# Graph attention layers: turn the state first, multiply by weights that carry two score columns, then attend; slope of the scores on ScalarE

## The chip, the cores and the metric

The kernel runs on one core of one Trainium2 chip, in one launch. The metric is the device time of the whole program in microseconds (us). The engines are named as in the profile: PE (TensorE, matrix products), PEld (its weight loads), DVE (VectorE), ACT (ScalarE), POOL (GpSimd) and SP (SyncE, which issues all DMAs here). Everything is computed in f32.

## What is computed

128 independent graphs have 128 nodes with 256 features each. Three attention layers follow one another, each with its own weights `W` and score vector `a`, and then a gated graph network with three steps:

```python
h = jnp.maximum(_layernorm(x, axis=-1), 0.0)
x = x + _L0_gnn_ref(h, adj, L0_gnn_W, L0_gnn_a)      # layers 1 and 2 alike

# _L0_gnn_ref(x, adj, W, a)
Wh = jnp.einsum('bnf,fo->bno', x, W)
a1, a2 = (a[:F_out, 0], a[F_out:, 0])
e = (Wh @ a1)[:, :, None] + (Wh @ a2)[:, None, :]
e = jnp.where(e > 0, e, ALPHA * e)                   # ALPHA = 0.2
attention = jnp.where(adj > 0, e, NEG_BIG)
attention = jax.nn.softmax(attention, axis=-1)
h_prime = jnp.einsum('bij,bjo->bio', attention, Wh)
return jax.nn.elu(h_prime)

# layer 3, three times: m = h @ weight[i]; aggr = A^T m; h = GRU(aggr, h)
```

## The kernel before

**Tiles and groups.** The graphs are taken in 33 groups: two graphs in the first and the last, four in the others (`SIZES`, L217). A tile has the nodes or the features on its 128 partitions. `gat(g)` (L670) loads a group's `x` and `adj`, makes the mask `cap` (a very large number where there is an edge, minus it elsewhere) and runs `attention(g, l, ...)` (L491) three times; it then normalises once more and turns the state so that the features are on the partitions (`h`). `gru(g, ...)` (L736) runs three steps with 24 products of 512 columns each (L790, names `nn`, `r`, `z`, `ni`) and the aggregation (`agp`, L813), writes the result and the output. A turned copy of the state for the next step (`hn`) goes out to DRAM and back through `turned_state` (L469).

**One attention layer** (group of n graphs). `stats` (L414) gives mean and 1/deviation on DVE and POOL. ACT makes `xn = relu((x - mean) * rs)` (L507). The scores are made from `xn` without the product `Wh`: at the start `attention_weights` (L286) computes `va = W a` for both halves of `a` on DVE (L304), spreads it over the partitions with PE transposes (`vp`, L309) and an ACT copy (L316), and each graph then costs two DVE instructions that multiply `xn` by `va` and sum along the row into `e` (L515). One of the two score columns must lie along the row: `de` takes it to DRAM (L537) and `er` brings it back to all partitions (L539). DVE adds both scores and takes the minimum with `cap` (L557), applies the slope with a second instruction (L569, maximum of em and 0.2 em) and takes the negative row maximum (L571); ACT computes the exponential with its row sum (L575); DVE divides (L582, L586). The attention matrix is turned through DRAM by `exchanged` (L438: DVE transposes 32 x 32 blocks, one DMA writes, four DMAs read back, `at`). PE multiplies `xn` by the attention matrix (`ahp`, L627: 8 products of 128 columns for four graphs), ACT copies the sum to SBUF (`ah`, L634), and PE multiplies it by `W` (`hp`, L646: two k halves of 256 columns per graph). The elu and the sum with x are L660, L662 and L664.

**Near and far.** Groups 0 and 1 are "near" (`FAR = 2`, L216): there, turning is done by PE transposes into PSUM (`e`, `atp`) in place of trips through DRAM, and `rs` is multiplied in later (L515, L606). All other groups are "far".

**The order of the work** is made once, when the program is built. `Plan` (L40) collects every instruction with its engine, an assumed duration and a rank; `issue` (L108) walks through time, gives each engine the lowest rank among what is ready within 0.1 us, holds back whatever is more than 6.0 ranks ahead, and lets an instruction start only when the ring of its buffers (mostly 2) has a free slot. Group g has the ranks 3g to 3g + 3 for its gates, and its attention starts `lead(g)`, 6.5 to 9.5, before that (L926), 2 ranks to a layer. DMAs are planned at 250 KB/us, one behind another, and 1.9 us (L162). The chip then runs each engine's list strictly in that order, each instruction waiting for its semaphores; SP's list of DMAs as well.

**PSUM.** Eight banks: two for everything of the attention (`gat`), five for the gates, one for turning (L235).

Of the kernel before, what the change touches and what calls it, by code (L numbers as in the profile page):

```python
# [8 lines left out]
FT = mybir.dt.float32  # L9
# [176 lines left out]
def kernel(  # L186
# [97 lines left out]
    W, VA = [], []  # L284

    def attention_weights(l, w, a):  # L286
        rank = 1.5 * l - 8.0
        wt, va = const_val(f"w_{l}", [KD, D]), const_val(f"va_{l}", [2, D])
        first = l - 11.2
        load(256, first, lambda: nc.sync.dma_start(  # L290
            wt.t, w.rearrange("(k p) o -> p k o", p=P)), writes=[wt])
        ar = val(su, "ar", [2 * D], f"ar_{l}")
        load(2, first - 0.1, lambda: nc.sync.dma_start(
            ar.t[:1, :], a.rearrange("n o -> o n")), writes=[ar])

        ab = bank("gat", f"ab_{l}")
        add("PE", pe(T), rank, lambda: nc.tensor.matmul(
            ab.t, ones[:1, :], ar.t[:1, :], start=True, stop=True), reads=[ar], writes=[ab])
        wa = val(su, "wa", [2, KD], f"wa_{l}")
        vp = bank("gat", f"vp_{l}")  # L300

        def one(s, k):
            scr = val(su, "scr", [D], f"scr_{l}_{k}_{s}")
            add("DVE", dve(D) + 0.08, rank, lambda: nc.vector.scalar_tensor_tensor(  # L304
                scr.t, wt.t[:, k, :], 1.0, ab.t[:, s * D : (s + 1) * D], op0=OP.mult, op1=OP.mult,
                accum_out=wa.t[:, s, k : k + 1],
            ), reads=[wt, ab], writes=[scr, (wa, (s, k))])
            c = s * KD + k
            add("PE", 0.11, rank, lambda: nc.tensor.transpose(  # L309
                vp.t[:, c * P : (c + 1) * P], wa.t[:, s, k : k + 1].to_broadcast([P, P]), ident  # L310
            ), reads=[(wa, (s, k))], writes=[(vp, c)])

        for s in range(2):
            for k in range(KD):
                one(s, k)
        add("ACT", act(T), rank, lambda: nc.scalar.copy(  # L316
            va.t.rearrange("p s d -> p (s d)"), vp.t), reads=[vp], writes=[va])
        W.append(wt)
        VA.append(va)
# [118 lines left out]
    def exchanged(srcs, cut, dst, name, n, rank):  # L438
# [7 lines left out]
            dram, f"d{kd}_{n}", 2,  # L446
            lambda: dram.tile([Q, 32, Q, f], FT, tag=f"d{kd}_{n}", name=f"d_{name}"),
# [21 lines left out]
    def turned_state(src, dst, name, n, rank):  # L469


        tr = val(gw, "trs", [G, P], f"tr_{name}", cut=n)
        d = plan.val(
            dram, f"ds_{n}", 2, lambda: dram.tile([n, P, P], FT, tag=f"ds_{n}", name=f"d_{name}")
        )
        add("DVE", dve(n * P), rank, lambda: nc.vector.transpose(
            tr.t.rearrange("p b j -> p (b j)"), src.t[:, : n * P]
        ), reads=[src], writes=[tr], takes=[d, dst])
        load(64 * n, rank, lambda: nc.sync.dma_start(d.t.rearrange("b p f -> p b f"), tr.t),
            reads=[tr], writes=[d])  # L480

        def back(j):
            load(16 * n, rank, lambda: nc.sync.dma_start(
                dst.t[j * 32 : (j + 1) * 32, : n * P].rearrange("c (m r) -> c m r", r=32),
                d.t[:, :, j * 32 : (j + 1) * 32].rearrange("b (q c) r -> c (b q) r", q=Q),
            ), reads=[d], writes=[(dst, j)])

        for j in range(Q):
            back(j)

    def attention(g, l, xt, cap, xo):  # L491

        name, n = f"{g}_{l}", SIZES[g]
        rank = 3.0 * g - lead(g) + 2.0 * l
        xn = val(gw, "xn", [G, D], f"xn_{name}", cut=n)
        e = val(gw, "e", [2, G], f"e_{name}")
        far = g >= FAR
        nm, rs = stats(xt, n, name, rank, [xn, e, xo, cap])


# [5 lines left out]
        def centred(b):  # L506
            add("ACT", 0.45, rank, lambda: nc.scalar.activation(  # L507
                xn.t[:, b, :], xt.t[:, b, :], AF.Relu, bias=nm.t[:, b : b + 1],
                scale=rs.t[:, b : b + 1] if far else 1.0,
            ), reads=[(xt, b), nm, *([rs] if far else [])], writes=[(xn, b)])  # L510


        def score(b, s):
            scr = val(gw, "scr", [D], f"scr_{name}_{b}_{s}")
            add("DVE", dve(D), rank, lambda: nc.vector.scalar_tensor_tensor(  # L515
                scr.t, xn.t[:, b, :], 1.0 if far else rs.t[:, b : b + 1], VA[l].t[:, s, :],
                op0=OP.mult, op1=OP.mult, accum_out=e.t[:, s, b : b + 1],
            ), reads=[(xn, b), rs, VA[l]], writes=[scr, (e, (s, b))])

        for b in range(n):  # L520
            centred(b)
        for b in range(n):
            score(b, 1)
            score(b, 0)
# [3 lines left out]

        em = val(gw, "em", [G, N], f"em_{name}", cut=n)
        if far:
            de = plan.val(
                dram, f"de{n}", 2, lambda: dram.tile([P, n], FT, tag=f"de{n}", name=f"de_{name}")
            )
            er = val(gw, "er", [N * G], f"er_{name}")
            load(2, rank, lambda: nc.sync.dma_start(de.t, e.t[:, 1, :n]),  # L537
                reads=[(e, (1, b)) for b in range(n)], writes=[de], takes=[er, em])
            load(64 * n, rank, lambda: nc.sync.dma_start(  # L539
                er.t[:, : N * n], de.t.rearrange("p n -> (p n)").partition_broadcast(P)  # L540
# [4 lines left out]
        def row(b):  # L545
            add("PE", 0.11, rank, lambda: nc.tensor.transpose(
                e2.t[:, b * P : (b + 1) * P], e.t[:, 1, b : b + 1].to_broadcast([P, P]), ident
            ), reads=[(e, (1, b))], writes=[(e2, b)], takes=[em])

        def e2_row(b):  # L550
            if far:
                return er.t[:, : N * n].rearrange("p (i b) -> p b i", b=n)[:, b, :]
            return e2.t[:, b * P : (b + 1) * P]


        def masked(b):
            add("DVE", dve(P) + (0.15 if far else 0.05), rank, lambda: nc.vector.scalar_tensor_tensor(  # L557
                em.t[:, b, :], e2_row(b), e.t[:, 0, b : b + 1],
                cap.t[:, b, :], op0=OP.add, op1=OP.min,
            ), reads=[er if far else (e2, b), (e, (0, b)), cap], writes=[(em, b)])  # L560
# [3 lines left out]
        for b in range(n):  # L564
            masked(b)
# [3 lines left out]
        add("DVE", dve(n * P), rank, lambda: nc.vector.scalar_tensor_tensor(  # L569
            em.t, em.t, ALPHA, em.t, op0=OP.mult, op1=OP.max), reads=[em], writes=[em])  # L570
# [18 lines left out]

        if far:  # L590

            at = val(gw, "at", [Q, G * 32], f"at_{name}")
            exchanged([em], lambda k: em.t, at, f"at_{name}", n, rank)
        else:
            atp = bank("gat", f"atp_{name}")
            at = val(gw, "at", [G, N], f"at_{name}", cut=n)
# [6 lines left out]
        if not far:  # L603
            for b in range(n):
                turn(b)
            add("DVE", dve(n * P), rank, lambda: nc.vector.tensor_tensor(  # L606
                at.t, atp.t[:, : n * P].rearrange("p (g i) -> p g i", g=n),
                rs.t.rearrange("p (g o) -> p g o", o=1).to_broadcast([P, n, N]), op=OP.mult,
            ), reads=[atp, rs], writes=[at])

        def turned_weights(b):
            if far:
                return at.t[:, :, : n * 32].rearrange("p q (b c) -> p b q c", b=n)[:, b]
            return at.t[:, b, :]

        def summed(ps, b):
            o = ps.t[:, b * P : (b + 1) * P]
            return o.rearrange("p (q c) -> p q c", q=Q) if far else o


        ah = val(gw, "ah", [KD, T], f"ah_{name}")

        def gathered(k):
            ps = bank("gat", f"ahp_{name}_{k}")

            def product(b):
                add("PE", pe(P), rank, lambda: nc.tensor.matmul(  # L627
                    summed(ps, b), xn.t[:, b, k * P : (k + 1) * P], turned_weights(b),
                    start=True, stop=True,
                ), reads=[(xn, b), at], writes=[(ps, b)], takes=[ah])  # L630

            for b in range(n):
                product(b)
            add("ACT", act(n * P), rank, lambda: nc.scalar.copy(  # L634
                ah.t[:, k, : n * P], ps.t[:, : n * P]), reads=[ps], writes=[(ah, k)])

        for k in range(KD):
            gathered(k)

        def pair(j):  # L640
# [3 lines left out]
            def product(b, k):  # L644
                c = 2 * j + b
                add("PE", pe(D), rank, lambda: nc.tensor.matmul(  # L646
                    hp.t[:, b * D : (b + 1) * D], ah.t[:, k, c * P : (c + 1) * P],
                    W[l].t[:, k, :], start=(k == 0), stop=(k == KD - 1),
                ), reads=[(ah, k), W[l]], writes=[hp], takes=[t])

            for b in range(2):
                for k in range(KD):
                    product(b, k)
# [16 lines left out]
    def gat(g):  # L670
# [54 lines left out]
        if g == 0:  # L725
# [5 lines left out]
            [hn] * KD, lambda k: hn.t[:, :, k * P : (k + 1) * P], hT, f"h_{g}", n, rank  # L731
# [4 lines left out]
    def gru(g, xt, am, hn0, h0):  # L736
# [36 lines left out]
        def step(i):  # L773
# [50 lines left out]
            def half(c):  # L824
# [58 lines left out]
                if i < STEPS - 1 and FAR <= g < NG - FAR:  # L883
                    ahead.append(state(f"hn{c}", f"hn_{g}_{i + 1}_{c}"))
                    turned_state(hc, ahead[c], f"hn_{g}_{i + 1}_{c}", n_g, quick)
# [11 lines left out]
        if far:  # L897
            exchanged(
                h, lambda k: h[k].t[:, :TG].rearrange("p (b j) -> p b j", b=n_g),
                o, f"o_{g}", n_g, rank,  # L900
# [68 lines left out]
```

## Time and profile before

| | |
|---|---|
| runs of the kernel, median (lowest to highest) | 2757.47 us (2755.29 to 2758.84), 3 runs |
| profiled execution, first to last instruction | 2756.0 us; 1.5 us below the runs' median, no other time is recorded for it |
| busy: PE, PEld | 2712.8 us (98%), 1569.7 us (57%) |
| busy: DVE, ACT, POOL | 2082.3 us (76%), 1280.4 us (46%), 293.7 us (11%) |
| granted PE clock, mean | 0.996 |
| DMA | 503,094 packets, 245.30 MB, 33.5% of 16 engines on the one queue of SP |
| chain of work that ended last | PE 88%, DVE 8%, ACT 2%, DMA 1% |

A line of the groups gives source line, engine, operation, what is written and read, the shapes, the count, then busy us, the mean ns of one, and the idle time of the engine just before them with what ended it. An f32 product stands as two instructions on PE. Matmuls overlap in the pipeline, so the mean of one is longer than the distance between two starts.

### The profile page before, as it was taken

How to read it: one execution, taken by the hardware profiler on the slowest of the kernel's cores; microseconds unless marked ns; L12 is line 12 of the kernel's file. 1: busy time of each engine (PE TensorE's matmuls, PEld its weight loads, DVE VectorE, ACT ScalarE, POOL GpSimd, SP SyncE). 2: the span in 40 equal slices, each digit the busy share in tenths (PEclk: the TensorE clock that was granted, in tenths of full speed). 3: DMA queues.
4: the chain of work that ended last, by engine and by line, in shares of the span. 5: the costliest groups of instructions: out<-in, count | busy, mean ns of one | idle time of the engine just before them, and what ended most of it. 6: DMA issues, size and time to landing. Idle time of an engine off the chain costs nothing.

```text
span 2756.0 us, 32248 instructions
## 1 busy us (share of the span) xinstructions
PE 2712.8 (98%) x9563; PEld 1569.7 (57%) x9563; DVE 2082.3 (76%) x5541; ACT 1280.4 (46%) x2709; POOL 293.7 (11%) x369
## 2 busy tenths in 40 slices
PE   7899999999999999999999999999999999999998
PEld 4755555555555555555555555555555555555546
DVE  7778888778768887877788687778768886876643
ACT  4545444444444454444454445444444444444433
POOL 1111110101101101110111111111101010100000
PEclk9999999999999999999999999999999999999999
DMA  3113334433324433333333344323334333333310
GB/s 91 51 58 100 88 95 101 111 94 86 97 80 108 108 99 78 101 91 96 105 97 83 87 105 104 109 75 91 97 88 110 103 93 86 94 74 93 79 44 12
DMA packets 503094, 245.30 MB, mean 89 GB/s; under 512 B 280580, under 2 KB 472068, under 8 KB 502919
## 3 DMA queue, kind: packets, MB, share of 16 engines
q1 hardware_dynamic: 502918, 243.25, 33.5%
q8 instruction: 76, 1.25, 0.2%
q14 instruction: 100, 0.81, 0.1%
HBM read 139.28 MB, written 103.87 MB: 88 GB/s over the span
## 4 chain that ended last, share of the span: by engine, by line
PE 88%; DVE 8%; ACT 2%; DMA 1%; issue 1%; POOL 0%; SPq 0%; DVEq 0%; ACTq 0%; POOLq 0%
PE z L790 21%; PE r L790 21%; PE hp L646 11%; PE ni L790 11%; PE nn L790 10%; PE ahp L627 6%; PE agp L813 5%; DVE em L557 1%; DVE scr L515 1%; DVE xo L662 1%; DVE xo L664 1%; DVE d L877 1%; ACT em L575 1%; DVE h L880 1%; DVE n L856 0%
## 5 line engine op out<-in xcount | busy, mean ns | idle before, releaser
L790 PE MATMUL nn<-h,whh 128*128 128x512 f32 (+1 forms) x792 | 395.6, 581 | 1.9 <-DVE h L880 1.9
L790 PE MATMUL r<-ag,wc 128*128 128x512 f32 (+1 forms) x792 | 395.2, 581 | 1.3 <-ACT ag L821 1.3
L790 PE MATMUL ni<-ag,wc 128*128 128x512 f32 (+1 forms) x792 | 394.4, 579 | 1.4 <-ACT ag L821 1.4
L790 PE MATMUL z<-ag,wc 128*128 128x512 f32 (+1 forms) x792 | 394.2, 579 | 0.0
L790 PE MATMUL z<-h,whh 128*128 128x512 f32 (+1 forms) x792 | 394.2, 579 | 0.0
L790 PE MATMUL r<-h,whh 128*128 128x512 f32 (+1 forms) x792 | 394.2, 579 | 0.0
L851 DVE SCALAR_TENSOR_TENSOR n<-r,wn 128x512 f32<-128x512 f32 (+1 forms) x198 | 132.6, 670 | 336.5 <-ACT r L848 336.0
L646 PE MATMUL hp<-w,ah 128*128 128x256 f32 x1536 | 373.2, 381 | 0.5 <-ACT ah L634 0.2
L646 PEld LDWEIGHTS hp<-w,ah 128*128 128x128 f32 x1536 | 290.1, 190 | 131.4 <-issue 95.7
L515 DVE SCALAR_TENSOR_TENSOR scr<-xn,va 128x256 f32<-128x256 f32 x732 | 266.4, 423 | 33.9 <-ACT xn L507 33.6
L848 ACT ACTIVATE r<-r,brz 128x512 f32<-128x512 f32 (+1 forms) x198 | 133.2, 673 | 284.3 <-PE r L790 282.0
L813 PEld LDWEIGHTS agp<-am,hn 128*128 128x128 f32 x1536 | 202.3, 191 | 85.7 <-issue 73.5
L790 PEld LDWEIGHTS ni<-ag,wc 128*128 128x128 f32 x792 | 149.8, 190 | 177.9 <-issue 171.0
L790 PEld LDWEIGHTS r<-h,whh 128*128 128x128 f32 x792 | 149.3, 190 | 169.4 <-issue 162.8
L790 PEld LDWEIGHTS z<-h,whh 128*128 128x128 f32 x792 | 148.7, 190 | 168.3 <-issue 158.3
L821 ACT COPY ag<-agp 128x512 f32<-128x512 f32 (+1 forms) x198 | 113.0, 571 | 263.2 <-PE agp L813 262.8
L790 PEld LDWEIGHTS z<-ag,wc 128*128 128x128 f32 x792 | 148.4, 190 | 142.4 <-issue 138.2
L575 ACT ACTIVATE em<-em,nmx 128x128 f32<-128x128 f32 x384 | 149.4, 391 | 168.2 <-DVE nmx L571 166.4
L790 PEld LDWEIGHTS r<-ag,wc 128*128 128x128 f32 x792 | 146.1, 190 | 135.4 <-issue 120.5
L627 PEld LDWEIGHTS ahp<-at,xn 128*128 128x128 f32 x1536 | 191.3, 195 | 49.4 <-issue 37.6
L813 PE MATMUL agp<-am,hn 128*128 128x128 f32 x1536 | 205.3, 275 | 6.4 <-ACT hn L802 3.9
L526 POOL TENSOR_SCALAR xo<-xo 128x1024 f32<-128x1024 f32 (+1 forms) x66 | 73.2, 1110 | 1215.6 <-DVE xo L664 989.8
(94 smaller groups left out, 3474.1 us busy)
## 6 DMA issues: line engine op xcount, KB each, us to landing
d_hn<-tr_hn SPq DMA_DIRECT2D x116, 256.0 KB, 2.4
hn<-d_hn SPq DMA_DIRECT2D x464, 64.0 KB, 2.3
er<-de SPq DMA_DIRECT2D x90, 256.0 KB, 3.9
d_at<-tr_at SPq DMA_DIRECT2D x90, 256.0 KB, 2.0
at<-d_at SPq DMA_DIRECT2D x360, 64.0 KB, 2.0
x<-in_x_dram SPq DMA_DIRECT2D x31, 512.0 KB, 4.4
d_h<-tr_h SPq DMA_DIRECT2D x31, 512.0 KB, 2.9
h<-d_h SPq DMA_DIRECT2D x124, 128.0 KB, 3.1
```

Source lines behind the costliest of these rows:

```text
L515: add("DVE", dve(D), rank, lambda: nc.vector.scalar_tensor_tensor(scr.t, xn.t[:, b, :], 1.0 if far else rs.t[:, b : b + 1], VA[l].t[:, s, ...
L526: add("POOL", 0.14 + n * D / 1070, rank, lambda: nc.gpsimd.tensor_scalar(xo.t, xt.t, 1.0, -1.0, op0=OP.mult, op1=OP.add), reads=[xt], writ ...
L557: add("DVE", dve(P) + (0.15 if far else 0.05), rank, lambda: nc.vector.scalar_tensor_tensor(em.t[:, b, :], e2_row(b), e.t[:, 0, b : b + 1] ...
L575: add("ACT", 0.42, rank, lambda: nc.scalar.activation(em.t[:, b, :], em.t[:, b, :], AF.Exp, bias=nmx.t[:, b : b + 1], accum_out=sm.t[:, b ...
L627: add("PE", pe(P), rank, lambda: nc.tensor.matmul(summed(ps, b), xn.t[:, b, k * P : (k + 1) * P], turned_weights(b), start=True, stop=True ...
L646: add("PE", pe(D), rank, lambda: nc.tensor.matmul(hp.t[:, b * D : (b + 1) * D], ah.t[:, k, c * P : (c + 1) * P], W[l].t[:, k, :], start=(k ...
L662: add("DVE", dve(T), rank, lambda: nc.vector.scalar_tensor_tensor(u(), hp.t, 0.0, u(), op0=OP.max, op1=OP.add), reads=[hp, *parts], writes ...
L790: nc.tensor.matmul(o, w.t[:, k, c * P : (c + 1) * P], m, start=start, stop=stop)
L813: nc.tensor.matmul(ps.t[:, b * P : (b + 1) * P], s, am.t[:, b, :], start=True, stop=True)
L821: add("ACT", act(TG), quick, lambda: nc.scalar.copy(t.t[:, :TG], ps.t[:, :TG]), reads=[ps], writes=[t])
L848: add("ACT", act(TG) + 0.1, quick, lambda: nc.scalar.activation(r.t[:, :TG], pr.t[:, :TG], AF.Tanh, bias=brz.t[:, cr : cr + 1], scale=0.5) ...
L851: add("DVE", dve(TG), quick, lambda: nc.vector.scalar_tensor_tensor(n.t[:, :TG], r.t[:, :TG], 1.0, wn.t[:, :TG], op0=OP.add, op1=OP.mult), ...
```

## The change

The layer is computed in the order of the reference: `Wh = xn W` first, then attention times `Wh`. The weight tile gets two more columns, `W a1` and `W a2` (`E = D + 2`), so one product gives `Wh` and both scores.

- `attention_weights` writes the sums into the weight tile; `vp`, `va` and `wa` go.
- `xn` is turned first: for far groups through DRAM by `turned_blocks` (the old `turned_state`, now for any number of 128-column parts), with tile `xT`; for near groups by PE transposes and ACT copies.
- `mapped(b)`: PE multiplies the turned features of one graph by `W` with 258 columns, in one PSUM bank, and ACT copies it to `wh`. The eight DVE instructions for the scores go.
- The second score column goes to DRAM as single values from `wh` (stride 258), in graph-major order.
- The sum of the scores and the slope are one ACT instruction per graph (`Prelu` with the other score as bias); DVE then takes the minimum with `cap` for the whole group.
- The attention matrix is turned by `turned_blocks` in place of `exchanged`; `ahp` and `ah` go; `hp` is one product of 256 columns per graph.
- `turned_blocks` and `exchanged` share the ring of their SBUF tile by size (`tr1`, `tr2`); their DRAM rings have names of their own.

```diff
-        wt, va = const_val(f"w_{l}", [KD, D]), const_val(f"va_{l}", [2, D])
+        wt = const_val(f"w_{l}", [KD, E])
...
-                scr.t, wt.t[:, k, :], 1.0, ab.t[:, s * D : (s + 1) * D], op0=OP.mult, op1=OP.mult,
-                accum_out=wa.t[:, s, k : k + 1],
+                scr.t, wt.t[:, k, :D], 1.0, ab.t[:, s * D : (s + 1) * D], op0=OP.mult, op1=OP.mult,
+                accum_out=wt.t[:, k, D + s : D + s + 1],
...
-    def turned_state(src, dst, name, n, rank):
+    def turned_blocks(src, views, dst, name, n, rank, kind):
+        kd = len(views)
+        m = kd * n
+        tr = val(gw, f"tr{kd}", [kd * G, P], f"tr_{name}", cut=m)
...
+        def blocks(k):
+            add("DVE", dve(n * P), rank, lambda: nc.vector.transpose(
+                tr.t[:, k * n : (k + 1) * n, :], views[k]()
+            ), reads=[src], writes=[(tr, k)], takes=[d, dst])
...
+        load(64 * m, rank, lambda: nc.sync.dma_start(d.t.rearrange("m p f -> p m f"), tr.t),
...
+            load(16 * m, rank, lambda: nc.sync.dma_start(
+                dst.t[j * 32 : (j + 1) * 32, : m * P].rearrange("c (m r) -> c m r", r=32),
+                d.t[:, :, j * 32 : (j + 1) * 32].rearrange("m (q c) r -> c (m q) r", q=Q),
...
-            add("DVE", dve(D), rank, lambda: nc.vector.scalar_tensor_tensor(
-                scr.t, xn.t[:, b, :], 1.0 if far else rs.t[:, b : b + 1], VA[l].t[:, s, :],
-                op0=OP.mult, op1=OP.mult, accum_out=e.t[:, s, b : b + 1],
...
+            turned_blocks(
+                xn, [lambda k=k: xn.t[:, :, k * P : (k + 1) * P] for k in range(KD)],
+                xT, f"xT_{name}", n, rank, "xT",
...
+        def mapped(b):
+            ps = bank("gat", f"whp_{name}_{b}")
+            def product(k):
+                add("PE", pe(E), rank, lambda: nc.tensor.matmul(
+                    ps.t[:, :E], features(k, b), W[l].t[:, k, :], start=(k == 0), stop=(k == KD - 1)
+                ), reads=[xT, W[l]], writes=[ps], takes=[wh])
...
+                add("ACT", 0.45, rank, lambda: nc.scalar.copy(wh.t[:, b, :], ps.t[:, :E]),
...
-            load(2, rank, lambda: nc.sync.dma_start(de.t, e.t[:, 1, :n]),
+                    nc.sync.dma_start(de.t.rearrange("b p -> p b"), wh.t[:, :, D + 1])
...
-        def masked(b):
-            add("DVE", dve(P) + (0.15 if far else 0.05), rank, lambda: nc.vector.scalar_tensor_tensor(
-                em.t[:, b, :], e2_row(b), e.t[:, 0, b : b + 1],
-                cap.t[:, b, :], op0=OP.add, op1=OP.min,
+        def sloped(b):
+            add("ACT", 0.42, rank, lambda: nc.scalar.activation(
+                em.t[:, b, :], e2_row(b), AF.Prelu, bias=wh.t[:, b, D : D + 1], alpha=ALPHA,
...
-        add("DVE", dve(n * P), rank, lambda: nc.vector.scalar_tensor_tensor(
-            em.t, em.t, ALPHA, em.t, op0=OP.mult, op1=OP.max), reads=[em], writes=[em])
+        add("DVE", dve(n * P), rank, lambda: nc.vector.tensor_tensor(
+            em.t, em.t, cap.t, op=OP.min), reads=[em, cap], writes=[em])
...
-            exchanged([em], lambda k: em.t, at, f"at_{name}", n, rank)
+            turned_blocks(em, [lambda: em.t], at, f"at_{name}", n, rank, "at")
...
-                add("PE", pe(P), rank, lambda: nc.tensor.matmul(
-                    summed(ps, b), xn.t[:, b, k * P : (k + 1) * P], turned_weights(b),
...
-                    hp.t[:, b * D : (b + 1) * D], ah.t[:, k, c * P : (c + 1) * P],
-                    W[l].t[:, k, :], start=(k == 0), stop=(k == KD - 1),
+                    hp.t[:, b * D : (b + 1) * D], at.t[:, c * P : (c + 1) * P], wh.t[:, c, :D],
+                    start=True, stop=True,
```

## The prediction

> **What bounds the kernel now.** I read the busy time by stretches first, because an average over the span hides the two ends. The columns are the stretch, its length, then busy us (instructions) of PE, PEld, DVE, ACT and POOL, the granted PE clock, the DMA share and GB/s.
>
> ```profile
> 0.00:100.00 100.00, 75.29 (x328) 54.95 (x329) 73.75 (x267) 45.37 (x121) 17.65 (x30) 0.90 0.25 71
> 100.00:400.00 300.00, 294.81 (x1106) 179.95 (x1106) 236.31 (x655) 148.07 (x327) 34.30 (x44) 1.00 0.31 84
> 400.00:1400.00 1000.00, 999.04 (x3474) 569.00 (x3473) 782.54 (x2059) 471.81 (x989) 109.27 (x132) 1.00 0.36 95
> 1400.00:2400.00 1000.00, 999.25 (x3470) 568.32 (x3469) 781.73 (x2058) 470.49 (x985) 110.88 (x133) 1.00 0.36 95
> 2400.00:2756.00 356.00, 344.39 (x1193) 197.47 (x1191) 207.99 (x506) 144.66 (x290) 21.60 (x31) 0.99 0.24 63
> ```
>
> From 400 to 2400 us PE is idle for 1.7 us in all. DVE (78% there) and ACT (47%) have room. PE idles 24.7 us in the first 100 us, 5.2 us in the next 300 and 11.6 us behind 2400, 43 us altogether. So the time can move in three ways only: the sum of PE's work, the 30 us lost while the pipeline fills, and new stalls in the full part.
>
> PE's busy time is modelled, so I take the cost of a product from starts. The chain of waits in order of time (start, us, what) has two undisturbed runs:
>
> ```profile
> 111.88 1.78 PE ahp L627 x16
> 114.97 3.04 PE hp L646 x14
> ```
>
> That is 0.111 us for one 128-column instruction and 0.217 us for one of 256 columns (0.216 is the usual distance in the trace). The 512-column products start 0.429 us apart, so a column costs (429-216)/256 = 0.83 ns and 258 columns should cost 0.218 us. The groups by shape give the counts (two instructions for each f32 product) and the durations on the other engines:
>
> ```profile
> L646 PE MATMUL hp<-w,ah 128*128 128x256 f32 x1536 | 373.2, 381 | 0.5 <-ACT ah L634 0.2 <-DVE scr L304 0.2
> L627 PE MATMUL ahp<-at,xn 128*128 128x128 f32 x1536 | 193.8, 279 | 2.4 <-DVE at L606 1.7 <-DMA at<-d_at 0.6
> L515 DVE SCALAR_TENSOR_TENSOR scr<-xn,va 128x256 f32<-128x256 f32 x732 | 266.4, 423 | 33.9 <-ACT xn L507 33.6
> L557 DVE SCALAR_TENSOR_TENSOR em<-er,e,cap 128x128 f32<-128x128 f32 x366 | 155.9, 481 | 10.4 <-DMA er<-de 10.2
> L575 ACT ACTIVATE em<-em,nmx 128x128 f32<-128x128 f32 x384 | 149.4, 391 | 168.2 <-DVE nmx L571 166.4
> L507 ACT ACT_TABLE_LOAD x1 | 1.3, 1283 | 3.5 <-DMA x<-in_x_dram 3.5
> ```
>
> **PE, the bound.** Removed: ahp, 1536 x 0.112 = 172.0 us, and hp's 1536 x 0.216 = 331.8 us, 503.8 us together. Added: the mapped product, 128 graphs x 3 layers x 2 k x 2 = 1536 x 0.218 = 334.8 us, and the new pair product with one k, 768 x 0.216 = 165.9 us, 500.7 us together. In the two near groups (6 graphs) 36 transposes of xn come, 3.9 us at 0.109 us each, and the 12 of vp go, -1.3 us. Sum: **-0.5 us**. The products are only put in another order (weights first, attention second); the column count stays. In the full part this cannot move the time by more than 0.2%. The two PSUM banks of the attention serve six tiles a layer (four whp, two hp) where they served four; a whp tile holds its bank for 0.87 us of products and 0.37 us of copy, so PE finds the other bank free after its own 0.87 us or at most 0.4 us later: 0 to 1.6 us a layer, taken as 0 because gates' products stand between.
>
> **DVE.** The eight scores of a four-graph layer go: 266.4 us + 16.3 us of the near ones. The masked add goes: 155.9 + 5.6 us. The slope (L569, 695 ns) becomes a min with cap on the same 128x512, 0.69 us by the TENSOR_TENSOR of L856: nothing. Two transposes come for each far layer, 93 x 2 x 0.71 us (L451) = 132 us, and near the multiplication by rs goes, -3.4 us. DVE falls from 2082 to about 1767 us, 3.4 us less per layer. PE waits for DVE almost nowhere from 400 us on, so there this is worth nothing; where the pipeline fills it is worth something.
>
> **ACT.** Prelu comes 384 times; no row has it, and I take the Exp of the same tile with the same pointer bias, 391 ns (bounds: 242 ns of the 128-column copy at L332, 481 ns of the DVE row it replaces), 150 us. 384 copies of wh come at 371 ns (L634's 256 columns; 590 ns of L507 is the upper end), 142 to 227 us. ah's copies (113 us) go. ACT rises from 1280 to about 1470 us, 53%: hidden under PE, and queued in front of the gates' tanh by under 0.6 us at a time.
>
> On this tile the rows put ACT's 391 ns below DVE's 481. The Trainium skill (ScalarE: Activation LUTs, "Rules for kernel authors") says the opposite, that relu, max and min belong on VectorE, which is up to about three times faster per element in bf16. By that figure a Prelu would cost up to 3 x 481 = 1.4 us, an estimate from that page, and 384 of them 554 us; in f32 I go by the rows, and by either ACT stays below PE.
>
> No second table load stands in this trace, though the kernel mixes Relu, Copy, Identity, Exp and Tanh. If Prelu needed another table, each of 96 layers would switch twice, 96 x 2 x 1.283 = 246 us of ACT in front of the gates. The Trainium skill (ScalarE: Activation LUTs, "Table sets: the hidden batching unit") says that a load is paid at each change of set and names relu, not Prelu, for the set with exp and tanh; by that rule the rival is open, by the trace it can't be told.
>
> **DMA and latency.** These rows (size, median us from issue to landing) price the new trip:
>
> ```profile
> hn<-d_hn SPq DMA_DIRECT2D x464, 64.0 KB, 2.3
> d_h<-tr_h SPq DMA_DIRECT2D x31, 512.0 KB, 2.9
> h<-d_h SPq DMA_DIRECT2D x124, 128.0 KB, 3.1
> de<-e SPq DMA_DIRECT2D x90, 2.0 KB, 1.8
> bi<-in_L_gnn_b_ih_dram SPq DMA_DIRECT2D x1, 3.0 KB, 6.3
> ```
>
> xT is 512 KB out and four reads of 128 KB back: 2.9 + 3 x 0.48 (SP's issues, one behind another) + 3.1 = 7.4 us; behind them on SP stand hn's trips of the GRU. The score column is now a write of 512 single values where it was 128 rows of 16 B: between 1.8 us (de) and 6.3 us (bi, 768 single values, but in the crowded first 15 us); I take 2.3. The extra packets: 128 B ones take 12.7 ns and 512 B ones 29.2 ns in this trace, so xT adds (1024 x 29.2 + 4096 x 12.7)/16 = 5.1 us of 16 engines per layer, and at, whose reads shrink from 512 to 128 B, 0.7 us. 93 x 5.8 = 540 us lift the DMA share from 33.5 to some 53%: no bound.
>
> A far layer's latency: +1.4 (transposes) +7.4 +3.5 (16 mapped instructions) +0.4 (last copy) +0.5 (column), less 2.8 (eight scores 0.345 us apart), 1.8 (ahp), 0.6 (its copy) and 1.7 (half of hp) = **+6.3 us**, 19 us for three layers; against it 3.4 us less DVE queue per layer.
>
> Who waits for that latency? From group 5 on nobody: the turned state lands 30 us or more before its first gate product (group 12: the issue begins at 1030.1, the last of four lands by 1037, product at 1066.9). Group 2, the second line below, has no such margin: issue at 221.4, 4 us to landing, and its first gate product in the third line at 225.86.
>
> ```profile
> 70.25 1.09 PE L599 MATMUL atp<-ident,em 128*128 128x128 f32 x4 [6.79 <-DVE nm L697]
> 221.40 1.74 SPq L462 DMA_DIRECT2D h<-d_h  x4
> 225.86 1.02 PE L790 MATMUL nn<-h,whh 128*128 128x512 f32 x2
> ```
>
> The first line is the fill's longest idle time: PE stands 6.8 us with DVE working through two groups' softmax and statistics. Here the change helps: scores start without waiting for va (which came at 11 us), and a near layer loses 8 scores, ahp and its copy for two copies and a mapped product, about even in latency and 3 us lighter on DVE. I put the gain of groups 0 and 1 at 6 to 12 us. Group 2 starts earlier by that much, gains 3 x 3.4 us of DVE queue, and loses 19 us: -10 - 10 + 19 = about -1 us. Sum for the span of 2756.0 us: -0.5 (PE) -1 (fill) +0 (full part) = 2754.5; the runs shown have a median 1.5 us above the profiled span, so **2756 us**.
>
> **The rivals.**
> - *The fill gets shorter* (faster). If DVE's queue, over 78% busy between 100 and 400 us, is what delays group 2, then the 3.4 us per layer count more than once, since two layers queue side by side: half of the 30 us of idle goes, 2741 to 2750, say 2744. For it: the idle above ends on DVE. Against it: the far chain still gets four more transfers.
> - *Group 2 is late* (slower). The 6.3 us per layer come in full because the relief falls on other groups: from 221 us PE has no gates to do until the state lands, 3 x 6.3 = +19 us, 2775; with de at 6.3 us it is +31, 2787. It decides from the point at which group 2 lands more than about 2 us later than now. For it: the margin of 0.4 us. Against it: groups 3 and 4 have some 20 us of margin, so their products can fill.
> - *The full part stalls.* PE's order is fixed when the program is built, from planned landings of 250 KB/us; 128 B packets move 161 KB/us. If each far layer's first mapped product came 0.5 us late, with the gates' products queued behind it on PE, 93 x 0.5 = +46 us, 2803. Against it: hn has the same packets, and agp lost only 2.5 us to it in the whole run.
> - *Prelu costs table loads*: 246 us of ACT, partly on the gates' path, 2850 or more.
>
> **How the numbers follow.** The measurement tells apart about 0.2%, 5.5 us. Unchanged within that, 0.35 (2752 to 2763); fill shorter, 0.33; slower 0.32, of which group 2 late 0.22, stalls 0.08, table 0.02. The likeliest is 2756. For 8 in 10 I leave out the last two and a little of the others: 2738 to 2787.
>
> **What would show it.** Right: ahp and ah gone, PE's busy sum in 400:2400 still over 1995 us, 258-column products 0.218 us apart, one ACT_TABLE_LOAD, DVE near 1770 us. The rivals differ in 0:400, where PE's idle was 29.9 us, and in where group 2's first gate product stands (225.9 us now). Wrong: PE idle before mapped products behind 400 us, a 258-column product far from 0.218 us, or xT's reads landing after 5 us and more.

## The result, and the profile after

| | kernel before | changed kernel |
|---|---|---|
| median (lowest to highest), 4 runs each on one chip | 2758.15 us (2755.29 to 2759.0) | 3467.26 us (3462.33 to 3470.99) |
| ratio, 95% interval | | 1.2566 [1.2551, 1.2582] |
| profiled span | 2756.0 us | 3469.2 us |
| PE, DVE, ACT busy | 2712.8, 2082.3, 1280.4 us | 2930.7, 1813.7, 1419.4 us |
| granted PE clock, mean | 0.996 | 0.925 |
| DMA share of SP's queue | 33.5% | 55.8% |

The change makes the kernel 26% slower; I had forecast 2756 us with a range up to 2787. The span grew by 713 us. The busy time by stretches (stretch, length, then busy us of PE, PEld, DVE, ACT and POOL, granted clock, DMA share, GB/s) of the changed kernel:

```profile
0.00:100.00 100.00, 84.00 (x338) 59.55 (x339) 46.20 (x156) 59.21 (x162) 17.43 (x31) 0.91 0.29 79
100.00:400.00 300.00, 241.53 (x767) 143.66 (x765) 143.25 (x316) 119.70 (x284) 25.11 (x33) 0.90 0.47 86
400.00:1400.00 1000.00, 841.85 (x2464) 457.10 (x2464) 531.46 (x1092) 405.28 (x938) 79.92 (x102) 0.92 0.59 103
1400.00:2400.00 1000.00, 851.65 (x2526) 462.14 (x2525) 547.13 (x1120) 414.19 (x961) 83.08 (x104) 0.94 0.62 106
2400.00:3470.00 1070.00, 911.69 (x2729) 503.05 (x2727) 545.63 (x1119) 420.97 (x950) 75.91 (x100) 0.93 0.53 92
```

In the first 100 us PE is busy 8.7 us longer than before. Behind that it stands idle everywhere: 58 us of 300, then 158, 148 and 158 us of the next three stretches, where before it lost 1.7 us in 2000. No other engine is near its limit, and even in the fullest stretch the DMA engines are busy only 62% of the time. So PE waits for latency and not for an engine's throughput. The 218 us by which PE's busy sum rose are no new work: taken at the usual (median) distance between two starts of the same shape, the products add up to 2691.0 us now and 2691.2 us before.

What PE waits for stands in the groups (line, engine, operation, count, then busy us and the mean ns of one, then idle us before them and what ended it):

```profile
L549 PE MATMUL whp<-w,xT 128*128 128x258 f32 x1536 | 416.1, 403 | 124.2 <-DMA xT<-d_xT 118.9
L814 PE MATMUL agp<-am,hn 128*128 128x128 f32 x1536 | 249.7, 303 | 210.9 <-DMA hn<-d_hn 191.8
L593 ACT ACTIVATE em<-er,wh 128x128 f32<-128x128 f32 x366 | 120.5, 392 | 367.1 <-DMA er<-de 366.9
L648 PE MATMUL hp<-wh,at 128*128 128x256 f32 x768 | 212.7, 413 | 51.8 <-DMA at<-d_at 34.9
```

In all four lines most of the idle time ends on a DMA (the third is ACT's Prelu, the others are PE's products). The longest wait of PE is not in the attention at all: `agp` is the gates' aggregation, and `hn` its turned state, whose trip through DRAM the change kept; before, `agp` waited 2.5 us for it in the whole run. The DMA rows (count, size, median us from issue to landing) show which transfer is out of line:

```profile
hn<-d_hn SPq DMA_DIRECT2D x464, 64.0 KB, 3.4
d_o<-tr_o SPq DMA_DIRECT2D x30, 512.0 KB, 10.7
xT<-d_xT SPq DMA_DIRECT2D x360, 128.0 KB, 3.6
de<-wh SPq DMA_DIRECT2D x90, 2.0 KB, 9.8
```

The smallest of these, `de` with 2 KB, lands after 9.8 us, against 1.8 before. `d_o`, at 10.7, took 2.6 before; it is one of those that are held, as will be seen. The queue's own waits say what stands behind it (us in total, times, longest), first in the changed kernel, then in the one before:

```profile
SPq L578 <- DMA de<-wh: 696.0, 89, 12.0
```
```profile
SPq L539 <- DMA de<-e: 106.2, 79, 3.6
```

L578 and L539 are the issue of `er`. SP stood there 89 times for 696 us in all, where it was 106.2 us before. And SP's list from 1526 us on, with PE's wait at the end (start us, length, engine, line):

```profile
1526.77 0.38 SPq L574 DMA_DIRECT2D de<-wh  x1
1527.95 1.90 SPq L482 DMA_DIRECT2D hn<-d_hn  x4
1536.92 0.34 SPq L578 DMA_DIRECT2D er<-de  x1
```
```profile
1539.80 1.52 PE L814 MATMUL agp<-am,hn 128*128 128x128 f32 x8 [4.21 <-DMA hn<-d_hn]
```

`hn` was issued 1.2 us after `de`, on a transfer that took 2.3 us before; its products start 12 us after the issue. So a write of 2 KB delays in two ways: SP's list stands until it lands, and transfers issued right behind it are held with it. In the trace the 512 packets of `de` themselves are over, in the median, 1.2 us after the issue, at 8 ns each; the completion comes some 8 us later. Packets of other transfers that start between the issue of `de` and that of `er` take 977 ns on the mean against 181 ns elsewhere (4096 B, the writes of `d_o` and `d_h`), or 43 against 14 ns (128 B). The median does not move (159 and 13 ns in both): a few packets stand for long. Of the 4096 B ones 19% take over 1 us there, and none elsewhere.

### The profile page after: what moved, and what is told of

It reads as the page before. It is cut to its first block, busy times and chain, and to the rows that moved or that the text cites. A ratio compares the mean times of both kernels' runs of the same rounds, so it can differ in the third digit from the quotient of the medians.

```text
span 3469.2 us, 30032 instructions
## 1 busy us (share of the span) xinstructions
PE 2930.7 (84%) x8819; PEld 1625.5 (47%) x8819; DVE 1813.7 (52%) x3801; ACT 1419.4 (41%) x3294; POOL 281.4 (8%) x369
## 3 DMA queue, kind: packets, MB, share of 16 engines
q1 hardware_dynamic: 1187350, 339.22, 55.8%
## 4 chain that ended last, share of the span: by engine, by line
DMA 39%; PE 31%; DVE 14%; SPq 6%; ACT 5%; issue 4%; POOL 0%; DVEq 0%; POOLq 0%; ACTq 0%
DMA de<-wh 11%; PE z L791 7%; DMA hn<-d_hn 6%; PE whp L549 6%; PE r L791 6%; SPq L482 5%; DMA d_o<-tr_o 5%; DMA er<-de 4%; PE nn L791 3%; PE ni L791 3%; PE hp L648 3%; PE agp L814 3%; DMA d_hn<-tr_hn 3%; DMA xT<-d_xT 2%; DMA at<-d_at 2%
## 5 line engine op out<-in xcount | busy, mean ns | idle before, releaser
L549 PE MATMUL whp<-w,xT 128*128 128x258 f32 x1536 | 416.1, 403 | 124.2 <-DMA xT<-d_xT 118.9
L791 PE MATMUL nn<-h,whh 128*128 128x512 f32 (+1 forms) x792 | 433.1, 631 | 14.3 <-DMA h<-d_h 13.9
L549 PEld LDWEIGHTS whp<-w,xT 128*128 128x128 f32 x1536 | 298.2, 200 | 291.8 <-issue 201.4
L814 PE MATMUL agp<-am,hn 128*128 128x128 f32 x1536 | 249.7, 303 | 210.9 <-DMA hn<-d_hn 191.8
L814 PEld LDWEIGHTS agp<-am,hn 128*128 128x128 f32 x1536 | 235.1, 213 | 287.8 <-issue 255.2
L593 ACT ACTIVATE em<-er,wh 128x128 f32<-128x128 f32 x366 | 120.5, 392 | 367.1 <-DMA er<-de 366.9
L604 DVE TENSOR_TENSOR em<-em,cap 128x512 f32<-128x512 f32 (+1 forms) x99 | 66.7, 674 | 372.8 <-ACT em L593 372.8
L648 PE MATMUL hp<-wh,at 128*128 128x256 f32 x768 | 212.7, 413 | 51.8 <-DMA at<-d_at 34.9
L556 ACT COPY wh<-whp 128x258 f32<-128x258 f32 x366 | 132.0, 372 | 260.8 <-PE whp L549 254.4
L791 PEld LDWEIGHTS nn<-h,whh 128*128 128x128 f32 x792 | 155.5, 210 | 156.4 <-issue 151.8
```

The source lines that it names most:

```text
L549: add("PE", pe(E), rank, lambda: nc.tensor.matmul(ps.t[:, :E], features(k, b), W[l].t[:, k, :], start=(k == 0), stop=(k == KD - 1)), reads ...
L556: add("ACT", 0.45, rank, lambda: nc.scalar.copy(wh.t[:, b, :], ps.t[:, :E]), reads=[ps], writes=[(wh, b)])
L593: add("ACT", 0.42, rank, lambda: nc.scalar.activation(em.t[:, b, :], e2_row(b), AF.Prelu, bias=wh.t[:, b, D : D + 1], alpha=ALPHA,), reads ...
L648: add("PE", pe(D), rank, lambda: nc.tensor.matmul(hp.t[:, b * D : (b + 1) * D], at.t[:, c * P : (c + 1) * P], wh.t[:, c, :D], start=True, ...
L791: nc.tensor.matmul(o, w.t[:, k, c * P : (c + 1) * P], m, start=start, stop=stop)
L814: nc.tensor.matmul(ps.t[:, b * P : (b + 1) * P], s, am.t[:, b, :], start=True, stop=True)
```

## The experiments

The ratios are against the kernel before on the same chip. "Idle" is PE's, by the stretches.

### The column written as rows

The second score is first gathered by DVE, so that `de` is written as it was before, 128 rows of 16 B, and `er` is read node-major. All else is the changed kernel.

```diff
-                    nc.sync.dma_start(de.t.rearrange("b p -> p b"), wh.t[:, :, D + 1])
+            add("DVE", 0.16, rank, lambda: nc.vector.tensor_copy(e.t, wh.t[:, :, D + 1]), ...)
+            load(2, rank, lambda: nc.sync.dma_start(de.t, e.t), reads=[e], writes=[de])
```

> The changed kernel, with one thing put back: DVE gathers the score column of a far layer into a small tile (one instruction of 4 values a row), and the trip to DRAM writes 128 rows of 16 B as before, not 512 single values. Theory A (the write of single values takes some 8 us longer than planned, holds SP's queue and the packets of other DMAs, 90 times): this kernel stands at 2740 to 2790 us, the write lands in about 2 us, and PE is idle under 60 us. Rival B (the trips of xT, a longer chain and 128 B packets are what costs): above 3300 us. In between, say 3000 us, both share it.

Measured: 2854.52 us (2849.57 to 2857.94, 4 runs), 1.0339 [1.0322, 1.0356]; span 2856.2, `de` lands in 1.9 us. **613 us of the 713 were the way in which 2 KB are written.** But 100 us remain, and the run lies above the 2740 to 2790 us expected. The stretches show them, of this kernel and then of the one before:

```profile
100.00:500.00 400.00, 369.05 (x1201) 214.55 (x1201) 238.41 (x530) 201.12 (x456) 39.73 (x51) 0.96 0.51 111
500.00:2400.00 1900.00, 1859.16 (x5871) 1029.20 (x5870) 1262.10 (x2661) 1001.40 (x2227) 192.97 (x242) 1.00 0.58 130
```
```profile
100.00:500.00 400.00, 394.81 (x1455) 236.89 (x1455) 318.63 (x875) 196.52 (x429) 45.57 (x58) 1.00 0.32 87
500.00:2400.00 1900.00, 1898.29 (x6595) 1080.38 (x6594) 1481.94 (x3896) 893.85 (x1869) 208.87 (x251) 1.00 0.36 95
```

PE is busy 26 us less in the fill and 39 less in the full part. In the full part the granted clock is back at 1.00.

### The single values in the kernel before

The other way round: the kernel before, with nothing changed but the layout of `de`, written as single values in graph-major order, and the reading of `er` that goes with it.

```diff
-            load(2, rank, lambda: nc.sync.dma_start(de.t, e.t[:, 1, :n]),
+                    nc.sync.dma_start(de.t.rearrange("b p -> p b"), e.t[:, 1, :n])
```

> The kernel before, with the score column alone written as single values into a graph-major tile, all else as before (no xT, no mapped product). Theory A: the loss is there without the rest of the change, 90 times some 8 us on SP, 3300 to 3500 us, with the write landing after 8 us or more. Rival B: 2750 to 2790 us.

Measured: 3207.04 us (3206.36 to 3207.73, 2 runs), 1.1622 [1.1599, 1.1646]. The one line costs 448 us in a kernel whose products, DVE and ACT work are untouched; `de` lands in 9.0 us, and SP waits 651.7 us for it. The loss is there without the rest of the change, if below the 3300 to 3500 us expected. That it is less than 613 fits the lesser traffic, since there is no trip of `xT` to be held, but this was not tried by itself.

### The planner is told the price

Is the loss one of order, because the list was made for a write of 2.7 us? Here the planner adds 8 us to a DMA's usual time for it in place of 0.8; the chip does the same work in another order.

```diff
-            load(2, rank, column, more=0.8,
+            load(2, rank, column, more=8.0,
```

> The changed kernel, with only the planner's assumed landing of the single-value write raised by 7.2 us (from 3.2 to about 10.4 us), so that SP's and PE's lists are put in an order that expects it. Theory C (the write's length would be hidden if the order knew of it): back to 2760 to 2850 us. Theory A in its strong form (the write also holds the packets of whatever runs beside it, and SP waits in front of the read back in any order): 3000 us or more.

Measured: 3738.83 us (3738.28 to 3739.39, 2 runs), 1.355 [1.3523, 1.3577]. It is slower still, so that theory falls: a correct price doesn't help. PE's longest waits for DMAs suggest why (us in total, times, longest):

```profile
PE agp L814 <- DMA hn<-d_hn: 216.8, 46, 7.2
PE nn L791 <- DMA h<-d_h: 155.1, 17, 15.3
PE hp L648 <- DMA at<-d_at: 134.0, 34, 14.0
PE whp L549 <- DMA xT<-d_xT: 133.0, 24, 9.9
```

Now `h` and `at` are late as well. The planner put other transfers beside the write, in the time in which it took SP to be free: 174,598 packets of 128 B start between the issues of `de` and `er` (14.4 us apart in the median), where it was 74,913 (10.1 us). There they are held: in the 10 us after the issue of `de` 4096 B packets take 894 ns on the mean, and 177 elsewhere.

### Writes that nobody reads: neighbours, 16 B and 64 B apart

Does the write cost because `er` waits for it, or by itself? In the kernel before, each far layer also writes 512 scores as single values to a DRAM tile `dz` that nobody reads; `de` stays as it was. In two more kernels the same values lie 64 B and 16 B apart.

```diff
+                    nc.sync.dma_start(dz.t.rearrange("b p -> p b"), e.t[:, 1, :n])           # tile [n, P]
+                    nc.sync.dma_start(dz.t[:, :, 0].rearrange("b p -> p b"), e.t[:, 1, :n])  # [n, P, 16]
+                    nc.sync.dma_start(dz.t[:, :, 0].rearrange("b p -> p b"), e.t[:, 1, :n])  # [n, P, 4]
```

> The kernel before, whole, plus for each far layer one more write of the 512 scores as single values to a DRAM tile that nobody reads, so that no engine and no later DMA waits for it (only the write two layers on does, for its buffer). If the loss comes from SP standing in front of the read back: 2757 to 2790 us. If the write holds the packets of other DMAs: 2850 to 3150 us, with packets of 128 B near 50 ns behind such a write, where they took 13.

> As e6, but every value goes to a 64 B line of its own (stride 16 values). If the neighbours in one line are what makes the single values slow, the write lands in 2 to 3 us and the run is near 2757 to 2775; if any 4 B write is slow, it is like e6.

> As e6 and e7, the unread single values 16 B apart. At 4 B apart the write lands in 9.8 us, at 64 B in 3.5 us. If it goes by how many values share a 64 B line, four of them do here, where sixteen did: 4 to 6 us. If any sharing is as bad: above 8 us.

| single values | median us | ratio | `dz` lands after |
|---|---|---|---|
| neighbours (4 B apart) | 3036.15 (3032.45 to 3039.85, 2 runs) | 1.1006 [1.0984, 1.1028] | 9.8 us |
| 16 B apart | 2779.69 (1 run; before 2760.55) | 1.007, no interval | 4.3 us |
| 64 B apart | 2765.45 (2763.18 to 2768.82, 6 runs) | 1.0023 [1.0011, 1.0035] | 3.5 us |

The DMA rows of the first and of the last:

```profile
dz<-e SPq DMA_DIRECT2D x90, 2.0 KB, 9.8
```
```profile
dz<-e SPq DMA_DIRECT2D x90, 2.0 KB, 3.5
```

This settles it: with neighbours, a write that no engine waits for (of SP the profile puts three waits down to it, 10 us in all) costs 277 us, by what it holds up; the same number of packets of the same size and from the same places, 64 B apart, costs 6.5 us. In the two traces every engine and SP have the same instructions in the same order, so nothing but the addresses in DRAM is left. So the price is neither in the count of packets nor in the strided reading of SBUF, but in values that are neighbours in DRAM. What the memory does with them no trace shows, nor whether it matters that values share a line or that all 512 lie within 2 KB, since 64 B apart they spread over 32 KB. The Trainium skill (DMA: Bandwidth & Descriptors, "Specifications") says that below 512 B a transfer does a read-modify-write. That would fit values that share a stretch of memory, but it does not tell the three apart, since all of them, and the 16 B rows that land in 1.9 us, are below 512 B. Another rule there ("Rules for kernel authors") advises against a last dimension that isn't contiguous, because each element becomes a descriptor of its own; the advice is right here, though the count of descriptors is the smaller part of the price.

### What is left: four near groups

Group 2 is the first far one. With the column as rows, its first gate product still stands at about 254 us, against 225.9 before. Here groups 2 and 3 are near as well (and 6 far layers fewer are turned through DRAM).

```diff
-        far = g >= FAR
+        far = g >= 4
```

> As e1, and the attention of groups 2 and 3 is computed like that of the near groups, turned by PE in place of trips through DRAM (some 6 us more of PE). e1 is idle for 48 us of PE from 100 to 500 us, the kernel before for 10. Theory F (the longer chain of the first far groups starves PE while the pipeline fills): idle from 100 to 500 us falls under 20 us, the run to 2825 to 2840. If the fill isn't a matter of the trips: within 8 us of e1.

Measured: 2808.75 us (2808.67 to 2812.0, 4 runs), 1.0185 [1.0168, 1.0202], 46 us less than with the column as rows. The stretches:

```profile
100.00:500.00 400.00, 395.93 (x1373) 232.59 (x1373) 252.28 (x553) 221.05 (x502) 43.60 (x55) 1.00 0.42 99
500.00:2400.00 1900.00, 1864.89 (x5894) 1032.88 (x5893) 1264.78 (x2671) 1003.07 (x2224) 195.34 (x245) 1.00 0.58 130
```

The idle time of the fill is gone (4 us left of 31), and group 2's first gate product stands at 226.7. The run is better than the 2825 to 2840 us expected. The full part is still idle for 35 us. (The expectations for this kernel and the next two give PE's idle time higher than the profile does: from 100 to 500 us 48 for 31 with the column as rows and 10 for 5 in the kernel before, from 500 to 2400 us 61 for 41.)

### The reads priced higher

The planner counts 250 KB/us, but reads in 128 B packets move 161 KB/us. Is the rest of the loss in the full part due to that? First all reads of turned blocks are planned at the lower speed; then, with four near groups, those of `xT` and `at` only.

```diff
-            load(16 * m, rank, lambda: nc.sync.dma_start(
+            load(25 * m, rank, lambda: nc.sync.dma_start(
```

> As e1 (score column written as rows), and the planner takes the four reads back of a turned tile at 160 KB/us (12.7 ns for a 128 B packet on each of 16 engines), not at 250. e1 has some 61 us of PE idle from 500 to 2400 us, nearly all of it before the mapped products and before hp, where xT and at land. Theory D (these reads land later than the order expects): that idle falls under 25 us and the run to 2790 to 2825 us. Rival E (the DMAs of xT crowd the queue, whatever the order): within 10 us of e1's 2854.

> As e5 (four near groups, column as rows), and the planner takes only the reads of xT and at at 160 KB/us; those of hn keep the old price. In e4, where all three were priced, the idle before the mapped product and hp fell from 54 to 17 us (500 to 2400 us), and that before agp and nn rose from 8 to 29. If pricing hn did that: idle under 30 us here and the run near 2780. If the trips of xT crowd hn's whatever the order: idle stays near 45 to 55 us and the run at 2800 to 2810.

Measured: 2842.32 us (2835.96 to 2844.03, 4 runs), 1.0299 [1.0283, 1.0314], and 2846.51 us (2845.57 to 2850.39, 4 runs), 1.0313 [1.0298, 1.0329]. Both expectations were missed. The first is 12 us better than without the price: the waits of `whp` and `hp` between 500 and 2400 us fall from 37 to 8 us, those of `agp` and the gates rise from 4 to 18 (the expectation for the second kernel says 54 to 17 and 8 to 29). The second is 38 us worse than its base: there too `whp` and `hp` wait less for their DMAs and `agp` more (25.9 us for `hn` in the full part, 1.2 without the price). Pricing moves the waits from one consumer to another. Why the second is so much worse stays open.

### The traffic alone

The kernel before, with the trip of `xn` through DRAM in each far layer (512 KB out, four reads of 128 KB in 128 B packets) into a tile that nobody reads. DVE and PE do nothing for it. Two things change beside the traffic: all lists are made anew around the added transfers, and the scratch tile of the scores has one buffer in place of two, so that the scores no longer overlap (310.7 us of DVE, 266.4 before).

```diff
+            load(64 * m, rank, lambda: nc.sync.dma_start(xd..., xn...), reads=[(xn, b) ...], writes=[xd])
+                load(16 * m, rank, lambda: nc.sync.dma_start(xz..., xd...), reads=[xd], writes=[(xz, j)])   # j = 0..3
```

> The kernel before, whole, plus for each far layer the trip of xn through DRAM as the change makes it (512 KB out in rows of 512 B, four reads back in 128 B packets), without the transposes; no engine reads what comes back. It asks what of the 50 us that e5 still loses is the trip's traffic in itself. If the traffic crowds the trips of hn and at: 2785 to 2815 us, with agp waiting for hn. If the new waits (mapped product on xT) are the cost: 2757 to 2768 us.

Measured: 2834.24 us (2832.08 to 2836.71, 4 runs), 1.0265 [1.0248, 1.0282], 73 us, more than the 2785 to 2815 us expected for crowding; `agp` waits for `hn`, as expected. In its full part:

```profile
500.00:2400.00 1900.00, 1864.66 (x6422) 1047.57 (x6421) 1498.72 (x3811) 869.10 (x1827) 212.73 (x245) 1.00 0.55 130
```

This is the same 35 us of idle and the same 0.55 to 0.58 of DMA share as with four near groups, though nothing waits for the data. The victims are others. PE's longest wait here, and the two longest with four near groups:

```profile
PE agp L836 <- DMA hn<-d_hn: 33.1, 32, 2.9
```
```profile
PE hp L648 <- DMA at<-d_at: 20.6, 27, 1.6
PE whp L549 <- DMA xT<-d_xT: 13.6, 26, 0.9
```

Each is a sum of about 30 waits, of 2.9 us at most: what happens to be tight comes late. So the loss that is left in the full part is of the size that the traffic costs by its presence, on the DMA engines and as five more places on SP's list for each layer; which of the two was not told apart. Not all of it need be the traffic: the two kernels of the next section have the single scratch buffer without the trip, and PE idles there for 11 and 7 us in the same stretch.

### The new order for the near groups only

In the first 100 us PE had been busier, so groups 0 and 1 (in a second kernel 0, 1 and 2) get the new order, all others keep the old. To fit, `xT` takes the ring of `ah`, and `wh` and the scratch tile have one buffer in place of two.

```diff
-            attention(g, l, xt, cap, xo)
+            (attention_near if g < NEAR else attention)(g, l, xt, cap, xo)
```

> A mix: groups 0 and 1 in the new order (turned by PE, mapped product, Prelu), all far groups as in the kernel before, so no trip of xT and no single-value write. The part of the prediction on the fill: groups 0 and 1 gain 6 to 12 us; e1 was idle for 16 us of PE in the first 100 us where the kernel before was for 25. If that part holds: 2742 to 2752 us. If the far groups set the fill's end whatever comes before them: 2755 to 2765. Two small buffers are single here to make room, which could cost a few us.

> As e8, with group 2 in the new near order as well (12 layers' transposes more, 5 us of PE). If group 2's state is what PE waits for in the fill, below e8; if not, some 5 us above it.

Measured: 2789.01 us (2786.04 to 2790.31, 4 runs), 1.0104 [1.0087, 1.0121], and 2782.63 us (2781.82 to 2783.36, 4 runs), 1.0079 [1.0064, 1.0094]. The first lies 24 us above both ranges expected. The second is 6 us below the first, as expected for the case that PE waits for group 2's state. In the first 100 us PE has 285 and 284 instructions recorded, where the changed kernel has 338 and the one before 328; group 0's first gate product stands at 98.8 and 100.4 us, before at 80.1; and between 500 and 2400 us PE is idle for 11 and 7 us where it was 1.7. The single buffers differ too, so this says nothing sure about the order itself. No kernel tried here beats the one before.

## Why the prediction was wrong

**The step that failed** is the term "The score column is now a write of 512 single values ... between 1.8 us (de) and 6.3 us (bi, 768 single values ...); I take 2.3". It measured 9.8 us, above both bounds. `bi` is a read of single values from DRAM, and no row of the trace before showed a write of them; I took the direction to be without effect. And the term was booked in the wrong place. I charged it to a far layer's own latency, which has 30 us of margin from group 5 on. That margin is there (PE's products wait for `h` once in the run, 13.9 us), but SP's list is one for all: while it stands at `er`, or while transfers are held behind `de`, the gates' `hn` is late too, and that has no margin. The prediction had said that hn's trips stand behind `xT` on SP, and put no price on it. PE's own list is one as well: where a mapped product waits for `xT` (118.9 us), the gates' products behind it wait too. From the issue of `de` to that of `er` the changed kernel's SP takes 932 us in all, the one before 224, 708 us more; undoing the write gave 613 us of the time back.

**"From group 5 on nobody" waits, and a DMA share of 53% is "no bound".** The share was right (53.1% with the column as rows, 55.8% in the changed kernel), the conclusion wrong. The kernel with the unread trip loses 73 us at 55% in its full part. A mean share is no measure where each of PE's steps needs a small transfer soon after it is asked for. My rival of 46 us ("the full part stalls", 0.08) had the size and the place nearly right: with the column as rows the mapped products wait 26.8 us for `xT` and the pair products 28.6 us for `at` (14.3 and 19.9 of it in the full part). Its cause, the planned speed, is not confirmed: with the right price the waits moved and the time fell by 12 us once and rose by 38 the other time.

**Group 2 is late.** This rival came true, and my middle (the layers' gain pays for the latency) did not. These lines of the changed kernel answer to those of the prediction:

```profile
68.88 1.08 PE L632 MATMUL atp<-ident,em 128*128 128x128 f32 x4 [3.92 <-DVE em L621]
283.08 1.02 PE L791 MATMUL nn<-h,whh 128*128 128x512 f32 x2
```

The idle time before `atp` fell from 6.79 to 3.92 us, and PE is busy 8.7 us longer in the first 100. But that is work of any group, and not the gain of 6 to 12 us that I had put on groups 0 and 1: group 0's first gate product comes 1.4 us earlier (78.8 us for 80.1), group 1's 6 us later (140.6 for 134.4; 136.7 with the column as rows). By the gates' starts that gain is not to be seen. And group 2's first gate product went from 225.86 to 283.08 us; with the column as rows it is at about 254, still 28 us late where the rival had said 19. Taking the far chain out (four near groups) gave 46 us.

**The sum of the difference**, by spans: 613 us the single values, 49 us the far chain in the fill (and six far layers' trips less), 51 us the rest. The first two are shown by runs that undo them. For the third there is only the nearest measure, the kernel with the unread trip: against the kernel before, PE is idle 34 us longer between 500 and 2400 us there, and 33 us with four near groups. With four near groups PE's busy sum is also 27 us higher (2739.7 for 2712.8 us), which was not taken apart.

**What held.** 258-column products start 0.217 to 0.218 us apart, 256-column ones 0.216; PE's sum stayed (2691.0 against 2691.2). Prelu takes 392 ns (391 taken), and the trace has one table load, so that rival is out (its sum had 96 layers; 33 groups have 99):

```profile
L504 ACT ACT_TABLE_LOAD x1 | 1.3, 1283 | 3.6 <-DMA x<-in_x_dram 3.6
```

DVE is at 1813.7 us (1767 forecast), ACT at 1419.4 (1470). By the rule of the Trainium skill that the prediction weighed (ScalarE: Activation LUTs, "Rules for kernel authors") Prelu would have been up to 1.4 us, by my estimate; in f32 the row decides, 392 ns on ACT against 481 for the DVE instruction. It is 514 ns where `er` is read with a stride of four values. The other sign that I had named, `xT` landing after 5 us and more, did not come (3.6 us); the wait showed in PE's idle time before the mapped products, 124.2 us. As 118.9 us of that end on `xT`, the two PSUM banks were rightly taken at about 0.

## What to carry to other kernels

Before a layout is changed, look at what each DMA writes, value by value: a write of 4 B values that are neighbours in DRAM cost far more here than its bytes, and it was paid by whatever shares its queue; gather the values on an engine first (here 0.15 us on DVE) or keep them apart. A latency may be charged to a chain that has margin only if nothing else stands behind it on the same list: price the DMA list as an engine, with all that waits in it. And no row for an operation means that the bounds must come from rows of the same direction, or be left wide.

## What the runs showed of the hardware

- A write of 512 values of 4 B from SBUF to DRAM lands after 9.8 us if they are neighbours, 4.3 us at 16 B apart (one run), 3.5 us at 64 B apart; the same 2 KB as 128 rows of 16 B take 1.9 us.
- While such a write is under way, packets of other transfers are held: 4096 B ones take 977 ns on the mean against 181 ns elsewhere in the changed kernel, 757 against 169 in the kernel before with single values; with the column as rows there is no such difference (161 and 169).
- The completion comes late: the write's own packets are recorded as finished 1.2 us after its issue (median), the issue that waits for it goes on 10.1 us after.
- The granted PE clock was lower where PE idled much: 0.90 to 0.94 in the changed kernel's stretches (PE idle for 15 to 20% of them), 1.00 in the full part of every version with the column as rows (1 to 2%). How much of the 613 us is the clock was not separated.
